# Cross-attention's scores computed once and transposed for exp, and its sums inverted on chip, in a fused two-block transformer kernel

## The chip, the cores and the metric

The kernel runs on one core of a Trainium2 chip. The metric is the device time of one execution in microseconds, the median of three runs. PE is the matrix engine (PEld its weight loads), DVE the vector engine, ACT the scalar engine, POOL the general engine, and SP the one that issues most DMAs. The kernel holds PSUM as eight tiles of 128 x 512 float32, its banks; every matmul of the kernel writes to one of them, and its result must be read out by DVE or ACT before the bank is used again.

## The reference

Two transformer blocks follow one another on x of 2 batches x 1024 tokens x 256 channels, all in float32, with 16 heads of 16 channels. What is computed, cut to its core:

```python
# layer 0
x = x + mha(ln(x), ln(x))            # self-attention, 1024 keys a batch
x = x + mha(ln(x), ln(ctx))          # cross-attention, 64 keys a batch
x = x + moe(ln(x))                   # 8 experts of 1024, the best 2 a token
# layer 1
x = x + mha(ln(x), ln(x))
x = x + mha(ln(x), ctx, mask)        # scores + (1 - mask) * -10000
x = x + mlp(ln(x))                   # 256 -> 1024 -> 256
```

Each mha projects queries, keys and values, takes softmax(q k / 4) over the keys, multiplies by the values, and projects the result. (The reference splits the batch differently in its two blocks; the kernel sees 2 batches with 64 context keys.)

## The kernel before, in words

**Self-attention** is the frame for all else. A layer has 128 cells. In a cell PE makes two slots of four matmuls: two scores "a" (L753: queries on partitions, for the largest score), which DVE reduces (L760), and two scores "b" (L764: keys on partitions, for the weights), which ACT turns into exp (L770). The four matmuls of a slot stand on four row groups of the PE array, 32 contraction rows each, and every one fills a PSUM bank. The "a" scores run ten cells ahead of the "b" scores (LEAD). After a cell, or after two, comes the product with the values (L815, four column groups), copied by ACT (L827) and added by POOL (L828). Where a head group's maxima are complete they are transposed (L708) and subtracted from the queries by DVE (L710).

**Banks.** The eight banks are handed out in rotation from a list; a bank goes back to the end of the list when its last reader has been issued. The next user of a bank waits on the chip for that reader.

**The stream.** All other work stands in a stream of tasks, Python generators that issue some instructions and then yield their estimated cost in microseconds. A positive yield lets the planner go on or stop; zero or a negative one puts the task off to a later cell. After each cell the planner takes steps from the stream until a budget is used up (a pace worked out from what the tasks still cost and when they are due, at least 2.5 us a cell in layer 0 and 1.1 in layer 1). So keys, queries, values, projections and the cross-attention of tokens that are already through self-attention stand between the cells. What is left after the last cell is issued in one run, partly beside the experts (layer 0) or the MLP (layer 1).

**Cross-attention** works in units of 512 tokens, four a layer. The head dimension of 16 is padded to 32 columns, so that queries and keys have 512 columns in four groups of 128. A unit has these steps (functions norm, weigh and share):

- queries: L1063, 8 matmuls of 512 columns, with the bias added by ACT (L1070);
- scores for the maxima: L1082, 16 matmuls of 256 columns, with queries on partitions, reduced by DVE (L1089) into spread_c, one bank a time;
- four transposes (L1103), a copy (L1105), and a subtraction of the maxima from the queries (L1108, on POOL while maxima of self-attention are still made, else on DVE);
- scores again, now with keys on partitions: L1124, 8 matmuls of 512 columns on two row groups, then exp (L1133);
- product with the values: L1141, with columns of ones, so that the sums of the weights come out beside the products; copy by ACT (L1149);
- the division: the sums go through DRAM. L476 sends them out of the copied tile to sums_c, L477 sends the whole tile to DRAM, L481 gathers the products from there, DVE inverts the sums (L492), L493 writes them to the DRAM tensor turns, L497 reads them back spread over 16 partitions a head (by_c), and L503 multiplies (on POOL or DVE);
- the projection (L432), added to x by DVE (L440).

The context's keys and values are made once a layer (context_task): keys L981, in layer 1 a row with the mask (L989), written by 16 small ACT or DVE operations into kbd, a block-diagonal tile (L1000, L1002); values L1009 into vbd (L1020).

Layer 0's last units are followed by the routing, the dispatch (L1226, L1336: rows sent to DRAM in the order of their experts), and by 23 expert slots (L1510 transposes, L1544 and L1574 matmuls).

## Time and profile before

| what | value |
|---|---|
| median of three runs | 1692.17 us (1688.58 to 1693.54) |
| profiled execution | 1687.93 us, span 1685.9 us, mean granted clock 0.982 |
| layer 0's self-attention cells | 61.4 to about 612 us |
| end of layer 0, experts, start of layer 1 | about 612 to 1006 us |
| layer 1's self-attention cells | 1006 to 1502 us |
| layer 1's tail | to the end |
| passes: L753, L764, L815 | 2048 each, 523.1, 501.2 and 260.7 us of busy time |
| passes: L1063, L1082, L1124, L1141 | 128, 256, 128, 128; 58.6, 59.2, 34.7 and 39.0 us |
| a cell with a product of four | 2.92 us; with a product of eight 3.77 us |
| the context of layer 0: cells 8, 9, 10 | 7.50, 4.01 and 14.45 us |
| layer 0, cells 79 to 92 (its second unit) | 68.2 us |

The profile page shows how long each engine is busy, which lines take that time, and which waits end last. A float32 matmul of the program is two instructions in the trace, here called passes; a transpose is one. Ends of matmuls are modelled, so neighbours overlap in the busy time; what a series costs is read from the starts.

In the rows of groups the columns are: line, engine, operation, output and inputs with their sizes, count; then busy time, mean nanoseconds of one; then the idle time of the engine before them and what ended it. In a timeline a row is: start, length, engine, line, and in brackets the idle time before it with its releaser. In the chain of waits a row is a piece of the path that ended last: start, length, engine or DMA, line.

### The profile page before, as it was taken

What the parts mean: (1) busy time and instruction counts of PE and PEld (TensorE: products, weight loads), DVE (VectorE), ACT (ScalarE), POOL (GpSimd) and SP (SyncE); (2) the same over time, 40 slices, a digit from 0 to 9 for tenths busy, and PEclk for the clock granted to TensorE, in tenths of its full rate; (3) what the DMA queues carried; (4) which work ended last, traced back from release to release, by engine and by line L of the source; (5) the groups of instructions that cost most, each with busy time, mean ns of one, the idle gap of its engine ahead of it and who ended that gap; (6) DMA issues with size and microseconds to landing.
All of it is one profiled execution on the core that took longest, in us unless ns stands there. A gap on an engine that the chain in (4) does not pass through costs nothing.

```text
span 1685.9 us, 26108 instructions
## 1 busy us (share of the span) xinstructions
PE 1615.0 (96%) x9522; PEld 849.4 (50%) x9522; DVE 977.4 (58%) x2137; ACT 923.5 (55%) x1783; POOL 391.4 (23%) x479
## 2 busy tenths in 40 slices
PE   7989999999999987898999989999999999999998
PEld 3333344344434435687888854344344344335666
DVE  5658856587687635252211475976767677744420
ACT  2367866666665662333322316876766865774421
POOL 3124322232443302022111114421311331300000
PEclk8799999999999999999999999999999999999999
DMA  4333410210210144348556512100110112111100
GB/s 141 120 127 109 177 34 20 58 50 16 78 39 14 39 131 163 117 155 274 170 193 199 184 57 64 31 26 14 39 33 27 52 40 73 33 61 56 54 24 25
DMA packets 69739, 139.91 MB, mean 83 GB/s; under 512 B 17764, under 2 KB 31848, under 8 KB 69224
## 3 DMA queue, kind: packets, MB, share of 16 engines
q1 hardware_dynamic: 65768, 128.04, 23.6%
q0 software_dynamic: 3456, 9.51, 1.5%
q8 instruction: 77, 1.26, 0.3%
q10 hardware_dynamic: 384, 0.66, 0.2%
q14 instruction: 54, 0.44, 0.1%
HBM read 81.19 MB, written 48.07 MB: 77 GB/s over the span
## 4 chain that ended last, share of the span: by engine, by line
PE 84%; DVE 6%; DMA 5%; ACT 2%; issue 1%; SPq 1%; POOL 0%; DVEq 0%; ACTq 0%; POOLq 0%
PE banks L764 16%; PE banks L753 13%; PE banks L815 13%; PE banks L1544 7%; PE banks L1574 7%; PE banks L630 4%; PE banks L1063 3%; PE banks L1712 3%; PE banks L432 3%; PE banks L1082 3%; DVE mx_s L760 2%; PE banks L600 2%; PE banks L1700 2%; PE banks L1141 2%; PE banks L1124 1%; PE banks L364 1%
## 5 line engine op out<-in xcount | busy, mean ns | idle before, releaser
L760 DVE TENSOR_REDUCE mx_s<-banks 128x1 f32<-128x512 f32 x1024 | 635.3, 683 | 269.3 <-PE banks L753 266.5
L770 ACT ACTIVATE pt_s<-banks 128x512 f32<-128x512 f32 x1024 | 530.8, 607 | 164.7 <-PE banks L753 152.5
L753 PE MATMUL banks<-KS,QS 16*128 16x512 f32 x2048 | 523.1, 627 | 8.1 <-ACT pt_s L770 4.7
L764 PE MATMUL banks<-qb_s,KS 32*128 32x512 f32 x2048 | 501.2, 615 | 6.0 <-DVE qb_s L710 3.9
L828 POOL TENSOR_TENSOR acc_s<-acc_s,part_s 128x512 f32<-128x512 f32 x137 | 174.0, 1270 | 430.2 <-ACT part_s L827 428.9
L764 PEld LDWEIGHTS banks<-qb_s,KS 32*128 32x128 f32 x2048 | 171.9, 184 | 198.8 <-DVE mx_s L760 115.0
L815 PE MATMUL banks<-pt_s,v_s 128*20 128x512 f32 x2048 | 260.7, 601 | 0.2 <-ACT pt_s L770 0.2
L753 PEld LDWEIGHTS banks<-KS,QS 16*128 16x128 f32 x2048 | 194.8, 186 | 85.3 <-issue 41.4
L1550 ACT ACTIVATE h_s<-banks,w_slot 128x256 f32<-128x256 f32 x160 | 67.2, 471 | 178.1 <-PE banks L1544 101.3
L1544 PE MATMUL banks<-xsT,w_slot 128*128 128x256 f32 x640 | 149.5, 386 | 0.7 <-ACT xsT L371 0.7
L1574 PE MATMUL banks<-w_slot,h_s 128*128 128x256 f32 x640 | 144.9, 383 | 0.0
L815 PEld LDWEIGHTS banks<-pt_s,v_s 128*20 128x20 f32 x2048 | 43.5, 98 | 184.6 <-ACT pt_s L770 130.5
L1544 PEld LDWEIGHTS banks<-xsT,w_slot 128*128 128x128 f32 x640 | 120.9, 193 | 23.2 <-issue 3.0
L1574 PEld LDWEIGHTS banks<-w_slot,h_s 128*128 128x128 f32 x640 | 121.8, 192 | 20.2 <-DVE mx_s L760 1.5
L827 ACT COPY part_s<-banks 128x512 f32<-128x512 f32 x152 | 91.4, 601 | 58.1 <-PE banks L815 46.0
L1583 DVE SCALAR_TENSOR_TENSOR ys<-banks,gate,b 128x256 f32<-128x256 f32 x40 | 19.3, 483 | 142.7 <-PE banks L1574 141.5
L1589 POOL DMA_INDIRECT results<-ys,to x40 | 38.6, 966 | 257.0 <-DVE ys L1583 229.4
L630 PE MATMUL banks<-xT_s,w_att 128*128 128x512 f32 x128 | 68.0, 667 | 0.0
L1063 PE MATMUL banks<-xT_c,w_att 128*128 128x512 f32 x128 | 58.6, 602 | 1.3 <-ACT xT_c L371 1.3
L1082 PE MATMUL banks<-kbd,q_c 128*128 128x256 f32 x256 | 59.2, 383 | 0.0
L1712 PE MATMUL banks<-w_ff,h_f 128*128 128x256 f32 x256 | 57.3, 379 | 0.0
L1700 PE MATMUL banks<-hT_f,w_ff 128*128 128x512 f32 x128 | 56.2, 592 | 0.0
(265 smaller groups left out, 1398.6 us busy)
## 6 DMA issues: line engine op xcount, KB each, us to landing
w_slot<-in_ff_w_dram SPq DMA_DIRECT2D x40, 576.0 KB
w_slot<-in_ff_w_dram SPq DMA_DIRECT2D x40, 514.0 KB
sorted_rows<-fill SPq DMA_DIRECT2D x36, 520.0 KB
whole<-acc_s SPq DMA_DIRECT2D x32, 256.0 KB
whole<-osb_c SPq DMA_DIRECT2D x32, 256.0 KB
xs<-sorted_rows SPq DMA_DIRECT2D x20, 260.0 KB
ot_s<-whole SPq DMA_DIRECT2D x16, 256.0 KB
by_s<-turns SPq DMA_DIRECT2D x16, 256.0 KB
```

The source lines that it names most:

```text
L630: nc.tensor.matmul(p, lhsT=w[:, at + k * D + pair * P : at + k * D + (pair + 1) * P], rhs=xT[b][:, k, blk * 512 : (blk + 1) * 512], start= ...
L753: nc.tensor.matmul(sc, lhsT=QS[h % 4][r, qc * P : (qc + 1) * P], rhs=K[r, kh * 512 : (kh + 1) * 512], start=True, stop=True,)
L760: return i, lambda: nc.vector.tensor_reduce(mx[h][:, qc, j, kh : kh + 1], sc, AX.X, ALU.max)
L764: nc.tensor.matmul(sc, lhsT=K[r, n * P : (n + 1) * P], rhs=QB[h][r, :], start=True, stop=True)
L770: nc.scalar.activation(pt, sc, AF.Exp, scale=SCALE)
L815: nc.tensor.matmul(o[32 * j : 32 * j + VW, :], lhsT=V[b][:, cell % 8, 4 * g + j, :], rhs=exps.pop((cell, j)), start=(cell == cells[0]), st ...
L828: helper().tensor_tensor(acc[h], acc[h], part, ALU.add)
L1063: nc.tensor.matmul(p, lhsT=w[:, X_Q + k * HP + g * P : X_Q + k * HP + (g + 1) * P], rhs=xT[:, k, :], start=(k == 0), stop=(k == 1),)
L1082: nc.tensor.matmul(p[:, n, :], lhsT=q[:, g, t * P : (t + 1) * P], rhs=kbd[:, g, b, :], start=True, stop=True,)
L1544: nc.tensor.matmul(ph[:, n, :], lhsT=w[:, at : at + P], rhs=xT[:, k, :], start=(k == 0), stop=(k == 1),)
L1574: nc.tensor.matmul(py, lhsT=h1[:, f, h * P : (h + 1) * P], rhs=w[:, f * D : (f + 1) * D], start=(f == 0), stop=(f == 7),)
L1712: nc.tensor.matmul(py[:, n, :], lhsT=h1[:, f, t * P : (t + 1) * P], rhs=w2[:, f * D : (f + 1) * D], start=(f == 0), stop=(f == 7),)
```

## The change

The padding of heads is gone: queries and keys take 256 columns, in two groups of 128 (eight heads each). kbd holds, for each row tile of 32 partitions (two heads), the keys of the first head in its 64 columns, those of the second in the next 64, the other head's rows being zero; four ACT operations with a scale of 0 or 1 a partition make it. Weights of cross-attention and context shrink from 1536 to 1024 columns.

The scores are made once, with queries on partitions: one step takes two row tiles of a group and, for four blocks of 128 queries, multiplies each with its two heads' keys (128 columns) into two banks. In layer 1 a matmul of one row adds the mask ahead of each. For each bank DVE reduces the largest score of every query and head and subtracts it while it copies to SBUF. Then PE transposes (128 x 128) and ACT takes exp. The product with the values stands on four column groups. Sums are made by matmuls with a constant selection matrix (picks), inverted by DVE straight from PSUM, spread to the heads' 16 partitions by another matmul with picks, and multiplied by DVE from PSUM. The DRAM tensors whole and turns are no longer used by cross-attention, nor POOL's subtraction and multiplication. The task costs become 17 and 5 (24 and 4 before); while self-attention's maxima are still made, every step puts the task off to the next cell.

The diff, cut to its core:

```diff
-        pk = pk.rearrange("p (g b k) -> p g b k", g=4, b=B)
-        for g in range(4):
+        pk = pk[:, : 2 * B * SK].rearrange("p (g b k) -> p g b k", g=2, b=B)
+        for g in range(2):
...
-        for g in range(4):
-            for j in range(4):
-                r = slice(32 * j, 32 * j + 32)
-                dst, bias = kbd[r, g, :, SK * j : SK * (j + 1)], cols[r, C_K[att] + g : C_K[att] + g + 1]
-                ...
-                    nc.scalar.activation(dst, pk[r, g], AF.Identity, bias=bias)
+        yield 1.0
+        for u in range(2):
+            for g in range(2):
+                bias = C_K[att] + 2 * u + g
+                nc.scalar.activation(
+                    kbd[:, g, :, u, :], pk[:, g], AF.Identity, bias=cols[:, bias : bias + 1],
+                    scale=cols[:, C_U + u : C_U + u + 1],
+                )
             yield 0.3
...
+        def scores(g, n):
+            got = [(r, *bank()) for r in (2 * n, 2 * n + 1)]
             for t in range(4):
+                for r, _, p in got if layer == 1 else ():
+                    at = slice(32 * r, 32 * r + 1)
+                    nc.tensor.matmul(
+                        p[:, t * P : (t + 1) * P].rearrange("p (u k) -> p u k", k=SK),
+                        lhsT=ones[at, :],
+                        rhs=mask_f[at, b * SK : (b + 1) * SK].unsqueeze(1).to_broadcast([1, 2, SK]),
+                        start=True, stop=False,
+                    )
+                for r, _, p in got:
+                    rows = slice(32 * r, 32 * r + 32)
+                    nc.tensor.matmul(
+                        p[:, t * P : (t + 1) * P],
+                        lhsT=q[rows, g, t * P : (t + 1) * P],
+                        rhs=kbd[rows, g, b].rearrange("p u k -> p (u k)"),
+                        start=(layer == 0), stop=True,
+                    )
+            for r, i, p in got:
+                ...
+                nc.vector.tensor_reduce(mx, p, AX.X, ALU.max)
+                nc.vector.tensor_tensor(
+                    sc.rearrange("p (c k) -> p c k", k=SK), p,
+                    mx.unsqueeze(2).to_broadcast(shape), ALU.subtract,
+                )
+                free.append(i)
+                less[g, r] = sc
+
+        def weights_turned(g, n):
+            for r in (2 * n, 2 * n + 1):
+                i, p = bank()
+                sc = less.pop((g, r))
+                for t in range(4):
+                    nc.tensor.transpose(p[:, t * P : (t + 1) * P], sc[:, t * P : (t + 1) * P], ident)
+                pt = pts[g, r] = pool.tile([P, 512], F32, tag="p1", name=f"pt_{name}{g}{r}", bufs=4)
+                nc.scalar.activation(pt, p, AF.Exp, scale=SCALE)
+                free.append(i)
+
+        def product(g):
+            i, o = bank()
+            for r in range(4):
+                nc.tensor.matmul(o[32 * r : 32 * (r + 1), :], lhsT=vbd[:, b, 4 * g + r, :],
+                                 rhs=pts[g, r], start=True, stop=True)
+            j, s = bank()
+            for r in range(4):
+                for c in range(4):
+                    nc.tensor.matmul(
+                        s[32 * c : 32 * (c + 1), :P],
+                        lhsT=picks[:, O_SUM + 32 * r : O_SUM + 32 * (r + 1)],
+                        rhs=pts[g, r][:, c * P : (c + 1) * P], start=(r == 0), stop=(r == 3),
+                    )
+            nc.scalar.copy(q[:, g, :], o)
+            inv = inverse[g] = pool.tile([P, P], F32, tag="inv", name=f"inv_{name}{g}", bufs=2)
+            nc.vector.reciprocal(inv, s[:, :P])
+            free.extend((i, j))
+
+        def divided(g):
+            i, p = bank()
+            for c in range(4):
+                nc.tensor.matmul(
+                    p[:, c * P : (c + 1) * P], lhsT=picks[:, O_HEAD + c * P : O_HEAD + (c + 1) * P],
+                    rhs=inverse[g], start=True, stop=True,
+                )
+            nc.vector.tensor_tensor(q[:, g, :], q[:, g, :], p, ALU.mult)
+            free.append(i)
+
+        cost = 1.9 if layer else 1.0
+        for step, args, us, wait in (
+            (scores, (0, 0), cost, None),
+            (scores, (0, 1), cost, -1.0),
+            (weights_turned, (0, 0), 1.3, None),
+            (scores, (1, 0), cost, None),
+            (weights_turned, (0, 1), 1.3, None),
+            (scores, (1, 1), cost, None),
+            (product, (0,), 1.75, None),
+            (weights_turned, (1, 0), 1.3, None),
+            (divided, (0,), 0.85, None),
+            (weights_turned, (1, 1), 1.3, -1.6),
+            (product, (1,), 1.75, None),
+        ):
+            step(*args)
+            yield us
+            if maxima[0]:
+                yield 0.0
+            elif wait:
+                yield wait
```

The share function then calls divided(1) and the two projections; the code that sent, gathered, inverted and spread through DRAM is taken out of weigh and share.

## Prediction

> **What bounds the kernel now.** I read the page's busy times first, then the busy time in stretches of 100 us, then the groups of instructions by shape, then the timeline at the places that the change touches, and last the chain of waits.

> ```profile
> PE 1615.0 (96%) x9522; PEld 849.4 (50%) x9522; DVE 977.4 (58%) x2137; ACT 923.5 (55%) x1783; POOL 391.4 (23%) x479
> PE 84%; DVE 6%; DMA 5%; ACT 2%; issue 1%; SPq 1%; POOL 0%; DVEq 0%; ACTq 0%; POOLq 0%
> ```

> PE is busy for 96% of the span and carries 84% of the chain that ended last: a pass of PE that is removed is time, as long as PE finds its next bank free. The stretches (columns: length, then busy us of PE, PEld, DVE, ACT and POOL, then granted clock) show where that holds:

> ```profile
> 200.00:300.00 100.00, 100.00 (x669) 46.10 (x666) 68.55 (x121) 63.78 (x122) 24.75 (x32) 1.00 0.15 41
> 600.00:700.00 100.00, 83.83 (x390) 50.96 (x383) 42.77 (x165) 47.70 (x90) 12.23 (x12) 0.93 0.41 139
> 700.00:800.00 100.00, 90.67 (x418) 76.61 (x417) 36.27 (x150) 30.27 (x66) 25.06 (x28) 0.97 0.61 207
> ```

> In the attention stages (first row) PE is full and DVE is at 69%. At the end of layer 0 (the other two) PE waits, at a lower clock: this stage is bound by a chain.

> **Prices.** The groups by shape (busy us, mean ns of one):

> ```profile
> L1082 PE MATMUL banks<-kbd,q_c 128*128 128x256 f32 x256 | 59.2, 383 | 0.0
> L1063 PE MATMUL banks<-xT_c,w_att 128*128 128x512 f32 x128 | 58.6, 602 | 1.3 <-ACT xT_c L371 1.3
> L1089 DVE TENSOR_REDUCE spread_c<-banks 128x8 f32<-128x512 f32 x64 | 42.1, 686 | 21.2 <-PE banks L1082 20.7
> L710 DVE TENSOR_TENSOR qb_s<-QS,banks 128x512 f32<-128x512 f32 x32 | 21.9, 683 | 7.5 <-PE banks L708 6.3 <-DMA KS<-stk_s 1.3
> ```

> A PE mean overlaps its neighbours, so I price by spacing in the chain: 16 passes of L1063 in 6.87 us (0.43 each, 512 columns), 24 of L1082 in 5.18 (0.216, 256 columns); 128-column passes and transposes take 0.11 (4 in 0.44). A matmul is two passes, a transpose one. Four row or column groups start 7 ns apart and run together. A DVE reduction or subtraction of 128x512 takes 0.68.

> PE per unit before: queries 6.9, scores for maxima 6.9, transposes 0.44, second scores with product 8.7 (tail, 1583.39 to 1592.12): **23**. After: queries 8 passes x 0.43 = 3.5; scores 4 steps of 16 passes x 0.11 over 2 row groups = 3.5 (layer 1 again 3.5 for the mask); 32 transposes 3.5; products and sums 1.75 + 1.75; quotients 16 x 0.11 = 1.8: **15.7 in layer 0, 19.2 in layer 1**. PE alone thus gains 7.3 or 3.8 a unit.

> **What the scores cost DVE.** Each new step fills two of the eight banks, and each bank is freed only after a reduction and a subtraction: 4 x 0.68 = 2.7 us. A cell of self-attention already needs four reductions (2.48 us), and its sixteen passes take PE 1.75. A one-bank step is in the trace:

> ```profile
> 1254.87 1.28 DVE L1089 TENSOR_REDUCE spread_c<-banks 128x8 f32<-128x512 f32 x2
> 1256.26 2.48 DVE L760 TENSOR_REDUCE mx_s<-banks 128x1 f32<-128x512 f32 x4
> 1257.27 1.91 PE L815 MATMUL banks<-pt_s,v_s 128*20 128x512 f32 x16
> ```

> Around it (1250 to 1283) the cells that follow take 4.0 to 4.2 instead of 3.77: one or two extra reductions cost 0.25 to 0.47 even beside a product. In the new step DVE needs 2.48 + 2.7 = 5.2, PE only 1.75 + 0.87 = 2.6 (2.6 + 1.9 with a product). Banks go round in order, so the second slot of the next cell needs these two: PE's queue, with that cell's exps behind, stands until the last subtraction. I put this stall at 2.3 us in layer 0 (2.6 in cells without a product, less in others) and 2.0 in layer 1, where the mask gives PE 0.87 more to do. Bounds: 0.7 (DVE recovers beside the products' 3.77 us cells) and 4.0 (all of 2.7 with two reductions unfinished). By the new order 19 such steps stand between cells: 4 in units 0 and 1 of each layer, 3 in unit 2 of layer 0.

> Switching between row tiles and full tiles costs too: the four transposes L1103 start at 303.63 and L764 at 304.22, 0.59 for 0.44 of work, so 0.15, and 0.2 where a marked idle of 0.76 to 0.85 of the weight loads surrounds it. Net three more switches a unit: +0.6.

> **The sum, part by part** (against the profiled execution, 1687.9):

> - Layer 0, units 0 and 1: each -7.3 + 4 x 2.3 + 0.6 = +2.5; **+5**. Unit 2, its part inside: 14.3 of PE (queries, maxima, transposes) become 8.7 (queries, scores, half the transposes), and three stalls come in: -5.6 + 6.9 + 0.3 = **+1.6**.
> - Layer 1, units 0 and 1: each -3.8 + 4 x 2.0 + 0.6 = +4.8; **+9.6**.
> - Layer 0's context (94 to 120 us, 26 for three cells): sixteen small evacuations on ACT hold the exps, which hold PE:

> ```profile
> 105.88 5.93 ACT L1002 ACTIVATE kbd<-banks,cols 32x128 f32<-32x128 f32 x16 [0.83 <-PE banks L981]
> ...
> 112.49 2.07 PE L753 MATMUL banks<-KS,QS 16*128 16x512 f32 x2 [4.71 <-ACT pt_s L770]
> ```

> PE waits 4.71, then works at clock 0.50 until about 119. Four evacuations at 0.36 to 0.6 take at most 2.4; the wait and the slow 7 us go, and 8 passes with them: **-8** (-5 to -10). What is late next is the copy of QS to its place (2.4 to 2.9).
> - Cell 102 (498.6 to 512.4, 13.8 us): DVE's xd_m L1226 (5.09) stands beside other work; the dispatch moves to other cells: **-3** (0 to -6).
> - End of layer 0. The chain runs through DRAM:

> ```profile
> 698.94 6.03 DMA turns<-sums_c
> 704.99 3.70 DMA by_c<-turns
> 708.79 0.70 DVE q_c L503
> ```

> Unit 3 takes 39.7 us from its queries to its projection; with 15.7 of PE and no turn through DRAM about 23. The self-attention's own chain ends at 637.8 as before. From there to the first expert slot that needs the last tokens (762.5) are 124.7 us; less the 16 of unit 3's chain (nearly the 10 of PE work removed there, plus PE's idle 1.9 and 3.3 at 703.8 and 706.3) I have **-16**. Bounds: -8 (PE's expert work alone fills what opens) and -25 (unit 2's earlier dispatch also removes the 6.9 idle at 650.5 and its clock of 0.50).
> - Layer 1's context: half the key passes, no mask rows: **-2.5**.
> - Layer 1's tail (units 2 and 3, from 1489): no cells wait, so DVE's 2.7 hides partly under the MLP: -2.8 each; of the DRAM turns (3.25 + 3.89, 3.09 + 4.19) PE's own matmuls hid nearly all, 2 are left: **-7.6**.

> Priced at nothing: the reciprocal of 128x128 from PSUM (nearest rows: 128x32 at 0.35 on DVE, so 0.35 to 1.4; I take 1.0), two a unit, in cells with 3.5 us of product passes, which hide it; uncovered, ten in the stream add 10. ACT's added exps equal those removed; 32-head subtractions and quotients leave POOL (26 of 1.3 us), which bounds nothing. Fourteen DMA issues a unit leave SP's queue, at 0.45 to 0.65 each, so the DMAs of self-attention behind them only start earlier. The selection table (327 KB) loads last at the start, where four weight tiles of 512 columns less (262 KB each) save more.

> Sum: 5 + 1.6 + 9.6 - 8 - 3 - 16 - 2.5 - 7.6 = **-20.9**, so **1667**. The three runs lie at 1688.6 to 1693.5 (median 1692.2), 4.2 above the profiled execution; the range holds that. About 5 us (0.3%) is what can be told from no change.

> **Rules weighed.** The rows show no clock loss after 2.64 us of waiting (1489.1: clock 1.00), but 0.50 after 4.71. [...]

> **Rivals.**

> 1. *DVE's work is hidden* (0.14). For it: DVE is only 69% busy in the stage, and cells with products leave it 1.3 each. Stalls of 0.7 instead of 2.2: -28 more, **1639** (1630 to 1650). Against: even single extra reductions showed as 0.25 to 0.47.
> 2. *DVE and the banks become the bound* (0.22): the two banks of a step come free 4.0 us after it, at 19 places, +34 more: **1701** (1687 to 1715). It decides from a stall of 3.3 a step (2.2 + 20.9/19), where the gain is gone. For it: DVE has 0.4 us a cell to spare against 2.7.
> 3. *Small passes don't run together* (0.08): at 128 columns two row groups (steps) and four column groups (sums) go one after another: 8 x 3.5 + 8 x 5.2 = +70, **1737**. Against: groups at 512 columns start 7 ns apart.

> My own case (0.56) spans 1650 to 1687. **Chances**: faster 0.56 + 0.14 = 0.70; rival 2 lies half within 5 us of no change, 0.10; slower 0.12 + 0.08 = 0.20. The range from 1634 to 1704 leaves out rival 3 (0.08), rival 2 above 1704 (0.06) and the lowest of rival 1 (0.03), and takes in a stall of 0.7 or 4.0.

> **What would show it.** PE idle or its weight loads waiting for the subtraction or for mx_s after each score step, some 2 us (rivals: below 1, or 4); cells of layer 0's unit 1 summing to about 70.7 us (68.2 before); no ACT wait of 4.7 at layer 0's context; layer 0's end without the two DMA pieces and some 16 shorter; score passes of two row groups starting together. I would be wrong first if the expert stage gave back what the chain gained: it has PE work in stock, and a chain that ends sooner then only meets that.

## The result, and the profile after

| | median | runs | profiled span | mean clock |
|---|---|---|---|---|
| before | 1690.84 us | 1688.58 to 1693.54 (4) | 1685.9 us | 0.982 |
| after | 1715.76 us | 1712.18 to 1720.08 (4) | 1712.1 us | 0.953 |

The ratio is 1.0148, with a 95% interval of 1.0122 to 1.0174. The change made the kernel 25 us slower; the forecast was 1667, the range ended at 1704. The page after shows hardly more than the mean clock:

```profile
PE 1651.0 (96%) x10682; PEld 891.4 (52%) x10682; DVE 1021.6 (60%) x2188; ACT 893.3 (52%) x1728; POOL 360.9 (21%) x453
PE 85%; DVE 11%; issue 2%; DMA 2%; ACT 0%; POOL 0%; SPq 0%; DVEq 0%; POOLq 0%; ACTq 0%
```

PE is busy for 36 us more, where the forecast's prices gave it 44 us less (4 x 7.3 + 4 x 3.8), and DVE's share of the chain is 11% instead of 6%; the DMA's fell from 5% to 2%, as it should with the trips through DRAM gone. The stretches of 100 us that were shown of before (length, busy PE, PEld, DVE, ACT, POOL, granted clock):

```profile
200.00:300.00 100.00, 99.60 (x652) 45.44 (x645) 67.16 (x119) 60.01 (x114) 24.24 (x32) 0.95 0.12 33
600.00:700.00 100.00, 92.62 (x630) 51.95 (x626) 60.88 (x189) 54.28 (x105) 14.76 (x14) 0.91 0.33 108
700.00:800.00 100.00, 97.48 (x541) 82.39 (x534) 38.46 (x156) 36.34 (x77) 24.39 (x27) 1.00 0.55 186
```

In the attention stage, where the clock was 1.00, it is now 0.95 (0.84 in 400 to 490). A busy PE at half clock looks the same in the column of busy time (422 to 425, below: 3.00 of 3.00 us at 0.50). What each operation costs is as priced:

```profile
L1093 DVE TENSOR_TENSOR sc_c<-banks,mx_c 128x512 f32<-128x512 f32 x64 | 44.2, 691 | 2.2
L1092 DVE TENSOR_REDUCE mx_c<-banks 128x8 f32<-128x512 f32 x64 | 43.6, 681 | 28.7 <-PE banks L1081 28.5
L1129 PE MATMUL banks<-pt_c,picks 128*32 128x128 f32 x512 | 16.9, 273 | 0.0
L1138 DVE RECIPROCAL inv_c<-banks 128x128 f32<-128x128 f32 x16 | 15.3, 955 | 24.0 <-PE banks L1129 19.8 <-ACT q_c L1136 4.2
```

The reduction and the subtraction take 0.68 and 0.69, the reciprocal 0.96 (1.0 taken). What they do to PE is seen at two successive score steps of layer 0's second unit, which start at 414.64 and 418.63, in the timeline (start, length):

```profile
416.56 0.69 DVE L1093 TENSOR_TENSOR sc_c<-banks,mx_c 128x512 f32<-128x512 f32 x1
417.30 1.12 PE L747 MATMUL banks<-KS,QS 16*128 16x512 f32 x2
417.88 0.69 DVE L1093 TENSOR_TENSOR sc_c<-banks,mx_c 128x512 f32<-128x512 f32 x1
418.62 0.69 PE L747 MATMUL banks<-KS,QS 16*128 16x512 f32 x1 [0.20 <-DVE sc_c L1093]
419.15 0.59 PE L747 MATMUL banks<-KS,QS 16*128 16x512 f32 x1
...
421.41 0.69 DVE L1092 TENSOR_REDUCE mx_c<-banks 128x8 f32<-128x512 f32 x1
421.49 2.08 PE L758 MATMUL banks<-qb_s,KS 32*128 32x512 f32 x3
422.14 0.69 DVE L1093 TENSOR_TENSOR sc_c<-banks,mx_c 128x512 f32<-128x512 f32 x1
422.75 0.68 DVE L1092 TENSOR_REDUCE mx_c<-banks 128x8 f32<-128x512 f32 x1
422.88 3.39 PE L747 MATMUL banks<-KS,QS 16*128 16x512 f32 x4
423.46 0.69 DVE L1093 TENSOR_TENSOR sc_c<-banks,mx_c 128x512 f32<-128x512 f32 x1
424.07 1.87 DVE L754 TENSOR_REDUCE mx_s<-banks 128x1 f32<-128x512 f32 x3
426.20 3.62 PE L809 MATMUL banks<-pt_s,v_s 128*20 128x512 f32 x16
429.75 1.84 PE L1106 MATMUL banks<-ident,sc_c 128*128 128x128 f32 x8
```

Each bank is given back only after its own subtraction. Behind the first step PE therefore gets the cell's four last score passes in two pairs, from 417.30 and from 418.62, and needs 2.44 us for them. Behind the second they go out from 422.88 and from 424.20. Then comes what the forecast left out: sixteen product passes take 3.62 us where they took 1.91 (before, 1257.27), and eight transposes 1.84 where they took 1.04 to 1.09 (288.06, 325.69). The granted clock in stretches of 3 us (length, busy PE, clock) says why:

```profile
416.00:419.00 3.00, 2.80 (x17) 1.00 0.25 89
419.00:422.00 3.00, 3.00 (x28) 0.85 0.14 47
422.00:425.00 3.00, 3.00 (x6) 0.50 0.59 212
428.00:431.00 3.00, 3.00 (x18) 0.50 0.09 33
431.00:434.00 3.00, 3.00 (x29) 0.95 0.01 3
```

From 421.1 to 431.4 PE has half its clock. The fall comes behind the first step's wait; the six passes in 422 to 425 are already slow. The trace's record of the clock shows this 18 times between 75 us and the last 5, in pieces of 3.4, 6.8, 10.2 or 13.7 us, 123 us in all; before it was 34 us in six pieces. The difference, 88 us at half clock, is some 44 us of time, an estimate that takes PE to have work throughout: without it the result would be about 1672.

Where the time went, by the starts of self-attention's cells:

| stretch | before | after | difference | forecast |
|---|---|---|---|---|
| to cell 8 (clock at the start) | 94.3 | 96.3 | +2.0 | 0 |
| cells 8 to 23, context | 62.8 | 52.7 | -10.0 | -8 |
| cells 23 to 52 | 116.2 | 119.7 | +3.5 | 0 |
| cells 52 to 79, unit 0 | 123.8 | 135.9 | +12.1 | +2.5 |
| cells 79 to 96, unit 1 | 80.0 | 95.0 | +15.0 | +2.5 |
| cells 96 to 109, dispatch | 59.8 | 54.0 | -5.8 | -3 |
| cells 109 to 127, part of unit 2 | 74.6 | 94.4 | +19.9 | +1.6 |
| end of layer 0, experts, layer 1's context | 394.6 | 362.5 | -32.1 | -18.5 |
| layer 1's cells to 183 | 212.4 | 214.7 | +2.3 | 0 |
| layer 1's cells 183 to 255 | 283.5 | 312.6 | +29.2 | +9.6 |
| tail | 184.0 | 174.2 | -9.8 | -7.6 |

The context went as described: four evacuations in two pairs, with the cell's exps between them, and cell 10 takes 3.9 us instead of 14.5.

```profile
103.82 0.81 ACT L987 ACTIVATE kbd<-banks,cols 128x128 f32<-128x128 f32 x2 [0.20 <-PE banks L975]
106.86 0.83 ACT L987 ACTIVATE kbd<-banks,cols 128x128 f32<-128x128 f32 x2
```

More than the whole miss stands in the four stretches with score steps between cells: 76.2 us instead of 16.2. Not all of that is score steps. In cells 109 to 127 PE stands idle for 7.2 us at 556.8, the longest of the four waits in this row (us in total, times, longest):

```profile
PE banks L358 <- DVE xn_c L346: 13.0, 4, 7.2
```

Here unit 2's layer norm (L346) stands on DVE behind some 30 small operations that lay out the expert slots (L1347 to L1420), and PE, which needs it next, then works at half clock from 564 to 571. Before, the same operations (550 to 556) stand beside query passes (L1063, from 548.87 and from 556.28), and no two starts of PE in this stretch are over 0.85 us apart. So some 11 of the 60 us above the forecast come from this meeting, not from score steps.

### The profile page after: what moved, and what is told of

The parts are those of the page before. It is cut to its first block, busy times and chain, and to the rows that moved or that the text cites. A ratio compares the mean times of both kernels' runs of the same rounds, so it can differ in the third digit from the quotient of the medians.

```text
span 1712.1 us, 28218 instructions
## 1 busy us (share of the span) xinstructions
PE 1651.0 (96%) x10682; PEld 891.4 (52%) x10682; DVE 1021.6 (60%) x2188; ACT 893.3 (52%) x1728; POOL 360.9 (21%) x453
## 4 chain that ended last, share of the span: by engine, by line
PE 85%; DVE 11%; issue 2%; DMA 2%; ACT 0%; POOL 0%; SPq 0%; DVEq 0%; POOLq 0%; ACTq 0%
PE banks L758 15%; PE banks L809 14%; PE banks L747 14%; PE banks L1538 8%; PE banks L1568 8%; PE banks L624 4%; DVE mx_s L754 3%; PE banks L1706 3%; PE banks L426 3%; PE banks L1694 3%; PE banks L594 2%; PE banks L1106 2%; DVE mx_c L1092 2%; PE banks L1051 2%; PE banks L358 1%
## 5 line engine op out<-in xcount | busy, mean ns | idle before, releaser
L764 ACT ACTIVATE pt_s<-banks 128x512 f32<-128x512 f32 x1024 | 533.0, 608 | 184.8 <-PE banks L747 129.6
L747 PE MATMUL banks<-KS,QS 16*128 16x512 f32 x2048 | 566.9, 651 | 7.2 <-DVE sc_c L1093 3.4
L758 PE MATMUL banks<-qb_s,KS 32*128 32x512 f32 x2048 | 519.7, 626 | 6.1 <-DVE qb_s L704 3.7
L822 POOL TENSOR_TENSOR acc_s<-acc_s,part_s 128x512 f32<-128x512 f32 x141 | 179.2, 1271 | 535.5 <-ACT part_s L821 534.8
L809 PE MATMUL banks<-pt_s,v_s 128*20 128x512 f32 x2048 | 282.5, 642 | 1.2 <-DVE mx_s L754 1.0
L758 PEld LDWEIGHTS banks<-qb_s,KS 32*128 32x128 f32 x2048 | 180.7, 187 | 180.7 <-DVE mx_s L754 97.3
L747 PEld LDWEIGHTS banks<-KS,QS 16*128 16x128 f32 x2048 | 204.6, 191 | 107.9 <-issue 40.5
L821 ACT COPY part_s<-banks 128x512 f32<-128x512 f32 x157 | 94.9, 604 | 99.6 <-PE banks L809 89.6
L1697 ACT ACTIVATE h_f<-banks,w_ff 128x512 f32<-128x512 f32 x32 | 22.0, 687 | 79.6 <-PE banks L1694 79.6
L1092 DVE TENSOR_REDUCE mx_c<-banks 128x8 f32<-128x512 f32 x64 | 43.6, 681 | 28.7 <-PE banks L1081 28.5
```

The source lines that it names most:

```text
L747: nc.tensor.matmul(sc, lhsT=QS[h % 4][r, qc * P : (qc + 1) * P], rhs=K[r, kh * 512 : (kh + 1) * 512], start=True, stop=True,)
L758: nc.tensor.matmul(sc, lhsT=K[r, n * P : (n + 1) * P], rhs=QB[h][r, :], start=True, stop=True)
L764: nc.scalar.activation(pt, sc, AF.Exp, scale=SCALE)
L809: nc.tensor.matmul(o[32 * j : 32 * j + VW, :], lhsT=V[b][:, cell % 8, 4 * g + j, :], rhs=exps.pop((cell, j)), start=(cell == cells[0]), st ...
L821: nc.scalar.copy(part, o)
L822: helper().tensor_tensor(acc[h], acc[h], part, ALU.add)
```

## The experiments

**The theory:** the waits of PE behind a score step make its clock fall to 0.50 for some 3 to 10 us, and this costs more than the waits. **Rival A:** the waits for DVE and the banks cost this time by themselves, the clock is a side effect. **Rival B:** PE's own new passes and switches cost it. The runs are not all from one chip; each ratio is to runs of the kernel before on the same chip.

**Useless work as a test.** A wait that is filled with passes that nobody needs cannot get shorter, but PE stays active.

```diff
+        def heat(times):
+            if maxima[0]:
+                for _ in range(times):
+                    nc.tensor.matmul(
+                        banks[:, free[0], :], lhsT=w[:, X_Q : X_Q + P], rhs=xT[:, 0, :],
+                        start=True, stop=True,
+                    )
...
                 less[g, r] = sc
+            heat(2)
```

> Two useless full-width passes pairs (two matmuls of 512 columns, 4 passes, 1.72 us) follow each score step that stands between cells, 19 steps: 33 us more work for PE. They write to the bank that the next slot overwrites. Theory (the waits of PE after a score step make its clock fall to 0.50, and that is what costs): the passes fill the wait, PE's clock stays up, time at half clock after the start falls from 123 us to under 60, and the kernel gets FASTER than the changed one: 1716 - about 30 to 44 of clock + little = 1675 to 1695. Rival A (the waits for DVE and the banks themselves cost, the clock is a side effect): the passes only fill the wait, 1716 within 6. Rival B (PE's own added passes cost): 1716 + 33 = 1749.

Measured: 1685.8 us, ratio 0.9951 (0.9929 to 0.9973) to the kernel before, where the changed kernel has 1.0148. Twenty steps stand between cells in the trace, not 19, so 80 useless passes were added, some 34 us, and they made the changed kernel 30 us faster. Half clock after 75 us is down from 123 to 55 us, 34 us of time. Rivals A and B fall. Unit 1 of layer 0 in the two kernels, changed and then with useless work (length, busy PE, clock):

```profile
404.60:499.60 95.00, 94.09 (x643) 0.87 0.09 26
```

```profile
398.50:484.10 85.60, 85.60 (x658) 1.00 0.09 29
```

The second has 6.9 us more work and is 9.4 us shorter, at clock 1.00.

The control has heat(2) at the end of weights_turned instead of scores, so the passes stand where no subtraction is waited for. The trace has 72 of them, some 31 us, as only two transposing steps of layer 0's unit 2 fall in the time when heat works.

> The control of the run before: the same useless passes, as many, but after the four transposing steps of each unit, where PE's next slot does not wait for the subtraction. Theory: the clock still falls after the score steps, the work is added: 1716 + 25 to 33 = 1741 to 1749, half clock as in the changed kernel (about 120 us). Rival A: the same, 1749. Rival B: 1749. Only the pair of runs tells: the theory wants the two apart by 50 or more, rival A by 33, rival B by nothing.

Measured: 1739.1, ratio 1.0261 (1.0236 to 1.0285), half clock 113 us. The pair is 53 us apart, as only the theory wants; the added 31 us cost 23, two below the expected band. Unit 1 there:

```profile
411.50:509.50 98.00, 96.39 (x659) 0.93 0.08 26
```

**Less work for DVE in a step.**

```diff
-                nc.vector.tensor_tensor(cut, p, mx.unsqueeze(2).to_broadcast(shape), ALU.subtract)
+                if maxima[0]:
+                    nc.scalar.copy(cut, p)
+                    nc.gpsimd.tensor_tensor(cut, cut, mx.unsqueeze(2).to_broadcast(shape), ALU.subtract)
+                else:
+                    nc.vector.tensor_tensor(cut, p, mx.unsqueeze(2).to_broadcast(shape), ALU.subtract)
```

> While self-attention's maxima are made, ACT copies each bank of scores to SBUF and POOL subtracts there, instead of DVE from PSUM; DVE has half the work in a step (1.36 instead of 2.7 us) and banks come free some 1.4 us earlier. Theory: the waits fall below what halves the clock at most steps; half clock under 70 us after the start, time 1716 - 19 x 1.36 - 30 = 1655 to 1675. Rival A: 1716 - 26 = 1690, half clock not what counts. Rival B: no change, 1710 to 1720.

Measured: 1676.4, ratio 0.9906 (0.9889 to 0.9922), half clock 65 us. 39 us less for 26 us less of DVE's work: the theory's side, a microsecond outside its band.

**The same work in another order.** In cells with a product the stream goes ahead of it, and a score step waits for such a cell.

```diff
-            if cell >= 2 and cell % 2 == 0:
-                product([c for c in (cell - 2, cell - 1) if c not in alone])
-                if owed < 2.5:
-                    continue
+            even = cell >= 2 and cell % 2 == 0
             most = 3.0
-            while owed > 0.6 and most > 0.0:
+            while owed > (2.499 if even and most == 3.0 else 0.6) and most > 0.0:
                 ...
+            if even:
+                product([c for c in (cell - 2, cell - 1) if c not in alone])
...
+            if step is scores and maxima[0] and place[0] % 2 == 1:
+                yield 0.0
             step(*args)
```

place[0] holds the number of the cell.

> Only the order is changed: in cells with a product the stream's steps come ahead of the product, and score steps between cells wait for such a cell, so that 0.9 to 1.9 us of product passes stand between a score step and the slot that needs its banks. DVE's work is the same. Theory: the wait shrinks from about 2.6 to about 1, the clock stays up at most steps, 1716 - 19 x 1.5 - 30 = 1660 to 1680. Rival A: -19 x 1.5 = 1688. Rival B: no change.

Measured: 1662.6, ratio 0.9813 (0.9787 to 0.9838), half clock 55 us. Not one instruction of cross-attention is changed, and 53 us are gone; the four stretches with score steps took 57 less, the end of layer 0 took 8 more. The timeline of a score step there:

```profile
417.70 1.32 PE L1081 MATMUL banks<-kbd,q_c 32*128 32x128 f32 x16
418.95 1.91 PE L810 MATMUL banks<-pt_s,v_s 128*20 128x512 f32 x16
420.80 0.70 PE L759 MATMUL banks<-qb_s,KS 32*128 32x512 f32 x2
...
422.31 1.13 PE L748 MATMUL banks<-KS,QS 16*128 16x512 f32 x4
423.37 1.09 PE L1106 MATMUL banks<-ident,sc_c 128*128 128x128 f32 x8
```

While PE makes the product (1.91), DVE is at the subtractions; the last four passes of the next cell go out in 1.13, not in 2.44 (or 3.39 at half clock). The weight loads' waits for the subtraction (us, times, longest), in the changed kernel and here:

```profile
PEld banks L747 <- DVE sc_c L1093: 31.4, 36, 1.0
```

```profile
PEld banks L748 <- DVE sc_c L1093: 13.9, 20, 1.0
```

None of them is longer than 1.0 us, in either. In the four stretches this kernel has +19.5 us against before, close to the 16.2 that the forecast had for them.

Both edits together:

> The new order of the score steps (ahead of a product) together with the subtraction on POOL behind a copy by ACT. Theory: with the waits already near 1 us, 1.4 us less of DVE's work per step removes what is left of them: 1662.6 - 19 x 0.5 = 1653, range 1645 to 1660; half clock after the start stays at 40 to 60 us, because what is left of it stands elsewhere. Rival A (only DVE's time counts, gains add up): 1676 + 1662.6 - 1716 = 1623 to 1635.

Measured: 1661.7, ratio 0.9800 (0.9778 to 0.9822), half clock 48 us. Rival A's sum fails by 27 us; but the 9 us that I still expected are not there either: with the order, DVE's share seems to have been covered already.

**Time or width of work?** The useless passes of the first experiment, with `lhsT=w[0:32, ...]` and `rhs=xT[0:32, 0, :]`:

> The useless passes after the score steps again, as many and as long, but with 32 contraction rows instead of 128, so that they work on one row group of PE only. If the clock follows time in which PE has something to do: as with full-width passes, 1686 (1678 to 1692), half clock under 70 us. If it follows how much of the array works: the clock falls as without them, half clock over 90 us, 1705 to 1745.

Measured: 1696.1, ratio 1.0001 (0.9985 to 1.0016), half clock 61 us. The clock stayed up nearly as with full-width passes (unit 1: 86.9 us, clock 0.98). The time is 4 us above the band, but not by the score steps: the four stretches with them took 613.3 us, and 612.5 with full-width passes (637.9 in the changed kernel). 6 us of the difference stand at the end of layer 0 (368.7 instead of 362.5), where neither kernel has added passes. So the clock followed time much more than width.

The clock's record tells the runs apart. Falls in the four stretches that start within 9 us of the start of a score step between cells:

| kernel | falls | us at half clock |
|---|---|---|
| changed | 12 | 75 |
| useless passes behind score steps | 0 | 0 |
| the same, 32 rows | 3 | 10 |
| useless passes behind transposing steps | 11 | 54 |
| subtraction on POOL | 4 | 17 |
| new order | 2 | 10 |
| new order and POOL | 1 | 10 |

The control's passes thus seem to have covered some of the waits, too, which fits its cost of 23 us for 31 of work.

**Is the order good for the kernel before?** The same change of order (without the wait for a cell, as there are no such steps):

> The kernel before with the stream's steps ahead of the product in cells with a product, nothing else. Its maxima steps take one bank and one reduction each. Theory: only the 0.25 to 0.47 a cell beside 25 score steps can be won: 1693 - 0 to 8 = 1685 to 1693. Rival (the order helps the whole stream, and not the new score steps): 1693 - 30 or more, as much as it gave the changed kernel beyond the score steps.

Measured: 1701.0, ratio 1.0025 (1.0009 to 1.0041). Neither was right: it loses some 4 to 6 us. In the profiled execution the end of layer 0 is longer (407.0 instead of 394.6, with 17 us more at half clock), while the cells take about what they took (495.5 instead of 495.9 in layer 1). The order alone wins nothing, so the 53 us that it gave the changed kernel belong to the score steps.

**The trips through DRAM alone**, in the kernel before:

```diff
-            osb = pool.tile([P, 512], F32, tag="osb", name=f"osb_{name}{g}", bufs=2)
-            nc.scalar.copy(osb, o)
+            nc.scalar.copy(q[:, g // 2, :], o)
             free.append(i)
-            return lambda: send(osb, pairs[g // 2], g % 2, sums[g // 2])
+            return lambda: None
...
-        gather(pairs[0], ot[:, 0, :])
-        invert(pairs[0], sums[0])
```

> The kernel before without cross-attention's way through DRAM: products are copied straight into the tile that is projected, and the gathering of heads and the division by the sums are left out. PE's work is the same. Theory (the forecast's share of the trips: the chain at the end of layer 0 and two idle us in the tail): 1693 - 6 to 12 = 1681 to 1687. Rival (the trips are what made the end of layer 0 32 us shorter in the changed kernel): 1693 - 20 to 25 = 1670.

Measured: 1686.7, ratio 0.9960 (0.9936 to 0.9985), 8.7 us less, in the theory's band. In the profile the end of layer 0 takes 386.7 us (394.6 before) and the tail 176 (184), but the cells from 52 on in layer 0 and those of layer 1 took 21 us more than before. The total is in the band partly by this, and the run leaves open why the cells grew.

**Layer 1's mask.** On the changed kernel, the order's kernel and the kernel with both:

```diff
-                for r, _, p in got if layer == 1 else ():
-                    ...
-                    nc.tensor.matmul(p[...], lhsT=ones[at, :], rhs=mask_f[at, ...], start=True, stop=False)
...
-                nc.scalar.activation(pt, p, AF.Exp, scale=SCALE)
+                shut = {"bias": mask_f[:, b : b + 1]} if layer == 1 else {}
+                nc.scalar.activation(pt, p, AF.Exp, scale=SCALE, **shut)
...
-        cost = 1.9 if layer else 1.0
+        cost = 1.0
```

> The changed kernel, with layer 1's mask given to ACT as the bias of exp (one value a key, keys being on partitions by then) instead of a one-row matmul ahead of every score matmul: 256 matmuls less, 0.87 us a score step. Theory: in the 8 steps between cells PE then only waits longer for the subtraction, and thinner work lets the clock fall more often; only the units in the tail gain, 2 x 3.5 = 7, perhaps less 10 of clock: 1716 - 7 to + 3 = 1709 to 1719. Rival B (PE's passes are what costs): 1716 - 14 = 1702.

Measured: 1704.4, ratio 1.0068 (1.0039 to 1.0096): 11 to 14 us less than the changed kernel, so rival B's total is nearer. The stretches say something else. Layer 1's cells from 183 on, in the changed kernel and here:

```profile
1225.30:1537.90 312.60, 306.40 (x2389) 0.97 0.09 27
```

```profile
1222.90:1550.30 327.40, 323.68 (x2388) 0.94 0.09 26
```

With less for PE to do, the cells took 14.8 us more at a lower clock; the tail took 151.9 instead of 174.2. Part of both is that the planner, told of cheaper steps, put more of unit 2 between the cells (24 score steps stand there, not 20). So this run does not tell theory from rival B.

> The same edit on the kernel with the score steps ahead of a product, where the product covers DVE's work: the gain should be whole, 7 in the tail and most of 7 between cells: 1662.6 - 9 to 14 = 1648 to 1654. Rival B: the same 1649.

Measured: 1645.8, ratio 0.9723 (0.9691 to 0.9755); 16.8 less than the order alone, three more than expected, and it stands in the tail (155.2 instead of 175.7), not between the cells (301.3 and 299.2).

> The same on the kernel with the order and POOL's subtraction: 1661.7 - 10 to 14 = 1648 to 1652, the best version.

Measured: 1637.6, ratio 0.9663 (0.9628 to 0.9697). This is the fastest version, 3.4% below the kernel before. It is better than expected by 10 us, and POOL's subtraction, worth nothing on top of the order alone, is now worth 8; why is open.

**What bounds the end of layer 0.** heat as in the first experiment, but with `if layer == 0 and not maxima[0]`.

> The changed kernel with useless passes only behind the score steps of layer 0's last unit, between the experts' work (8 matmuls, 16 passes of 0.43, 6.9 us, nearly what the change removed from PE in this unit). If PE's work is what bounds the end of layer 0 after the change, the stretch from the last cell of layer 0 to the first of layer 1 grows from 362.5 by 6 to 8, and the time to 1723. If a chain of waits bounds it (the self-attention's sums, the dispatch), it stays within 2 of 362.5, and the 32 us that it became shorter came from waits.

Measured: 1720.5, ratio 1.0159 (1.0129 to 1.0190). The stretch took 368.5 us, 6.0 more for 6.9 of work, as it should if PE's work bounds it. The stretch in the kernel before, in the changed one, and here (length, busy PE, clock):

```profile
611.50:1006.10 394.60, 368.13 (x1721) 0.97 0.51 169
```

```profile
648.10:1010.60 362.50, 352.01 (x1805) 0.99 0.53 176
```

```profile
646.20:1014.70 368.50, 359.20 (x1820) 0.99 0.52 173
```

The length alone does not show it: in the changed kernel and the five runs that leave this part as it is (both with passes in the cells of the score steps, the control, POOL's subtraction, the first with the mask) it was 362.5 to 368.7 us. But in these six PE was busy for 350.8 to 352.4 us and idle for 10.5 to 16.3; here it is busy for 359.2 and idle for 9.3. The idle time did not take up the added work, which speaks for PE. The total, 5 us above the changed kernel, is not clear of noise (ratios 1.0159 and 1.0148).

## Why the prediction was wrong

**The step that failed** is the price of a stall, 2.3 us for 2.3 us of waiting and nothing for the clock. It rested on one row, the idle 2.64 us at 1489 with clock 1.00, and on the 0.50 after an idle 4.71. The score steps have no idle as long as either, and still lose the clock: in unit 1 no two successive starts of PE at full clock are over 0.79 us apart, and no weight load waits over 1.0 us for the subtraction. A few passes go out as banks come free, and the clock fell all the same: of the 14 falls in the four stretches with score steps, 12 start within 9 us of such a step, and a fall slowed the product and the transposes behind the wait too (behind 421.1: 3.62 us for 1.91, 1.84 for 1.09). These 12 are 75 us at half clock, some 37 us of time; before there was none in these stretches. The first two experiments show that the clock is the cause: work added in the waits takes all 12 falls and 30 us away, nearly the same work added elsewhere does not.

**The clock ahead of its falls.** After 75 us half clock comes in pieces of 3.4 and 6.8 us before, and of 3.4, 6.8, 10.2 and 13.7 us in the changed kernel. In the kernel before, PE was nearly idle ahead of them: in the last 3.4 us, as long as the shortest piece, it started at most four passes before each of its six falls. Behind the score steps it was not: in the 3.4 us ahead of each of the 12 falls PE started 9 to 28 passes, no two of them over 0.79 us apart. How long or how thin a wait has to be for a fall was not shown. The forecast's sum has nothing for the clock; measured are some 37 us, for 12 falls of 6.3 us in the mean.

Point by point:

- *DVE's 2.7 us and the two banks as the limit of a score step*: right. Of the 60 us that the four stretches took beyond the forecast, some 37 are the clock behind score steps, 11 the layer norm's wait with its clock, and 3 a fall at 397.2 that no score step precedes; the 8 that are left make a step some 2.5 us where 2.2 was taken (an estimate, with the forecast's other terms as they stand), within the bounds of 0.7 and 4.0.
- *PE's prices*: right. Sixteen score passes go in 1.1 to 1.3 with their switch; groups of 128 columns run together (two row groups start 7 ns apart and a pair every 0.105 us, four column groups 6 to 8 ns apart and the next four after 0.109), so the third rival falls.
- *Context -8*: measured -10. *Tail -7.6*: -9.8. *Dispatch -3*: -5.8.
- *The layer norm's wait in cells 109 to 127*: +11, and no term of the sum had it. The forecast priced what moves off PE, not which DVE work would then meet.
- *End of layer 0, -16 and -2.5*: the place was right, the size too small, 18.5 of the 32.1 measured. PE's busy time fell by 16.1 us (some 10 of passes, the rest clock) and its idle time by 16.0 (26.5 to 10.5); I had counted 5 of idle. In the kernel without the trips alone, the stretch is 7.9 us shorter and its idle time 4.0. That PE's work bounds what remains is what the added work speaks for. How much of the remaining idle time went because dispatch began while cells were delayed was not tried.
- *Rival 2* (1701, waits of 4.0) came nearest in time, and not by its mechanism: the waits were about 2.5, the rest was mostly clock.
- The sum without the clock, about 1672, lies 5 us from the forecast; that is partly luck, as some +8 in the waits and +7 in the layer norm's wait stand against -14 at the end of layer 0.
- *Its signs*: cells 79 to 92 took 82.0 us where 70.7 was forecast. The forecast looked for its error first in the expert stage, which gave more than it was asked for.

## What to carry to other kernels

A wait of PE had two prices here: its own length, and half speed (clock 0.50) for whatever ran in the next 3.4 to 10.2 us. Before a step is placed, count what its readers (here DVE, 2.7 us on two of eight banks) hold back in the next slot, and put work of another kind, already due, between the step and that slot: the order alone turned +1.5% into -1.9%. Where the granted clock of a stage falls below 1.00, fill the waits with useless passes once, as a test: if the kernel gets faster, the clock is what it pays for.
